# A graph layer on one core: rows of B made from nodes in the order they lie, and the rest of the prologue beside a larger first chunk

## The chip, the cores and the metric

The kernel runs on one core of one Trainium2 chip. The metric is the device time of one execution in microseconds (us). The engines are PE (TensorE: matmuls; its weight loads are listed apart as PEld), DVE (VectorE), ACT (ScalarE), POOL (GpSimd) and SP (SyncE, which here only issues transfers). ACT and POOL issue transfers as well. Each engine works through its own list of instructions in order.

## What is computed

A graph network layer with a normalisation ahead of it and a residual sum behind it, on 12,500 nodes of 64 features and 212,500 edges that are sorted by `dst`:

```python
h = jnp.maximum(_layernorm(x, axis=-1), 0.0)
edge_in = jnp.concatenate([h[row], h[col], dist], axis=1)     # row = src, col = dst
e = jax.nn.silu(edge_in @ eW1 + eb1)
e = jax.nn.silu(e @ eW2 + eb2)
agg = jax.ops.segment_sum(e, row, num_segments=h.shape[0])
node_in = jnp.concatenate([h, agg], axis=1)
out = jax.nn.silu(node_in @ nW1 + nb1) @ nW2 + nb2
return x + out
```

The weights are 129 x 128 (eW1), 128 x 128 (eW2), 192 x 128 (nW1) and 128 x 64 (nW2); all are float32.

## The kernel before

The first edge layer is split: `h[src] @ eW1[:64] + eb1` is the table A (`ta`), `h[dst] @ eW1[64:128]` the table B (`tb`), one row per node, each row stored as three bfloat16 parts that add up to the float32 value. Nodes are kept in buckets: node n belongs to bucket n mod 100 at place n / 100, so a partition holds 100 consecutive nodes.

**Prologue (L201 to L319).** All of x is loaded with 100 consecutive nodes in a partition. For five groups of 20 buckets the norm is computed (L234 to L248), then for every four buckets the transposes (L252), the matmuls, and the three parts of B's rows (`product`, L169 to L192, called with s=1). Beside it the edge lists are prepared: for each pair of blocks the lowest `dst` (L267), the offset of each edge from it, bucket and place of each `src` (L282 to L293), the three parts of the edge weights (L298), and transposed copies (L301 to L313). `rows`, `aux`, the table `tb` and the transposed norms `hd` are written to HBM. The framework schedules this part.

**Blocks and chunks.** A block is 1024 edges. For each block `load` fetches `bc` (the offsets and buckets, copied to all partitions), a window of 112 rows of `tb`, and `pick` (edge weights). `count` (DVE) marks each edge's row and bucket and ranks the edges of a bucket by a running sum (L400). `send` multiplies the window by the marks (L435: 24 matmuls), copies the result to `qs`, and POOL scatters 128 rows at a time with an indirect transfer (L454) into a list `q` in HBM that is sorted by bucket of `src`. There are 208 blocks, eight scatters each (1661 in all). Blocks come in chunks, and each chunk has its own `q`: `CHUNKS` at L49 gives pairs of blocks, tiles of 128 rows per bucket and the rows that need no zero fill. Before, the first chunk has 8 blocks and one tile per bucket, and ten chunks of 20 blocks and two tiles follow. The fill of the next chunk's list is issued on ACT's queue (L96).

**Steps.** The lists are read back per four buckets (a batch; `fetch`, L489) together with A's rows. A step handles four tiles of 128 edges: mark the place of each edge (L521, L526), transpose the rows and add A's (L535, L542), Silu, second edge layer (L573), Silu, and sums per node (L587). One tile per bucket gives one step per batch, two tiles give two, so there are 525 steps in both versions.

**The order.** From L363 on the order of PE, DVE, ACT and SP is written out by hand. Ahead of the steps, `send_all(0)` sends the first chunk's blocks (L642). In the loop at L658 each turn calls the stages of several steps in the order of `turn` (L605), which has four hooks (`None`). At a hook pieces of the next chunks' blocks are run, three pieces to a block. `marks` spreads the pieces evenly over the hooks between two bounds: chunk c has to be sent when batch c x 25 - 5 is worked off, as its first batches are fetched then. A's rows are made by `feeds` (L623): `hd` is read back four buckets at a time, two calls of `next(feed)` per piece in the first chunk, then one per hook. `fetch` waits for a batch's A rows.

**Last chunk.** With its batches, `node_in` loads x and `hd`, and after a batch's sums `nodes` (L333) computes the node layers of four buckets, one stage per hook: two matmuls each into `z` (L341, L342), Silu, `o` (L346 adds the bias by a matmul with ones, L348), the sum with x (L351) and the store.

Of the kernel before, what the change touches and what calls it, by code (L numbers as in the profile page):

```python
# [48 lines left out]
CHUNKS = [(4, 1, 48)] + 10 * [(10, 2, 152)]  # L49
# [8 lines left out]
def tile_gnn(ctx: ExitStack, tc: tile.TileContext, x, src, dst, ew, eW1, eb1, eW2, eb2, nW1, nb1, nW2, nb2, out):  # L58
# [44 lines left out]
    CH = 20  # L103
    x_rows = x.rearrange("(l b) d -> l b d", b=NB)
# [24 lines left out]
    nb2r = const.tile([1, G, D], F32, name="nb2r")  # L129
    for t in range(G):  # L130
        nc.gpsimd.dma_start(nb2r[:, t, :], rows_of(nb2, 1))
# [35 lines left out]
    tables = [t.rearrange("(l b) f -> l b f", b=NB) for t in (ta, tb)]  # L167

    def product(s, b0, hr, ps, tag, sb, sb2, queue):  # L169
# [22 lines left out]
        queue.dma_start(tables[s][:, b0 : b0 + G, :], parts.rearrange("p b s f -> p b (s f)"))  # L192
# [4 lines left out]
    base_i = const.tile([1, 2, NP], I32, name="base_i")  # L197
    NW = 4
    wins = [const.tile([P, 3, H], BF16, name=f"win{i}") for i in range(NW)]

    with tc.tile_pool(name="pro", bufs=1) as pro, tc.tile_pool(name="norm", bufs=2) as np_, tc.tile_pool(  # L201
        name="nab", bufs=2
    ) as nab, tc.tile_pool(name="nps", bufs=2, space=PSUM) as nps:
        xs = pro.tile([P, NB, D], F32, name="xs")
        for c0 in range(0, NB, CH):
            nc.vector.memset(xs[96:, c0 : c0 + CH, :], 0.0)
            rows16(nc.sync.dma_start, xs[:, c0 : c0 + CH, :], x_rows[:, c0 : c0 + CH, :])
        for f in fill(0, nc.sync, NB):
            f()


        srcR = pro.tile([NP, PAIR], I32, name="srcR")
        dstR = pro.tile([NP, PAIR], I32, name="dstR")
        ewR = pro.tile([NP, PAIR], F32, name="ewR")
        pad_i = pro.tile([1, PAD], I32, name="pad_i")
        nc.gpsimd.memset(pad_i, N)
        pad_f = pro.tile([1, PAD], F32, name="pad_f", tag="pad_i")
        nc.gpsimd.memset(pad_f, 0.0)
        vec = lambda v, lo, n, m: bass.AP(tensor=v.tensor, offset=v.offset + lo, ap=[[m, n], [1, m]])
        for to, v, pad in (  # L220
            (dstR, dst, vec(dst, E - PAD, 1, PAD)),
            (srcR, src, pad_i),
            (ewR, ew, pad_f),
        ):
            for p0, p1 in ((0, NP // 16 * 16), (NP // 16 * 16, NP - 1)):
                nc.scalar.dma_start(to[p0:p1, :], vec(v, p0 * PAIR, p1 - p0, PAIR))
            nc.scalar.dma_start(to[NP - 1 : NP, :LAST], vec(v, (NP - 1) * PAIR, 1, LAST))
            nc.scalar.dma_start(to[NP - 1 : NP, LAST:], pad)


        hT = pro.tile([P, NB // 2, P], F32, name="hT")
        for c0 in range(0, NB, CH):
            xc_ = xs[:, c0 : c0 + CH, :]
            mean = np_.tile([P, CH], F32, name="mean")  # L234
            nc.vector.tensor_reduce(mean, xc_, AX.X, OP.add)
            nc.vector.tensor_scalar(mean, mean, 1.0 / D, None, op0=OP.mult)
            cen = np_.tile([P, CH, D], F32, name="cen")
            nc.vector.tensor_tensor(cen, xc_, mean[:, :, None].to_broadcast([P, CH, D]), op=OP.subtract)
            sq = np_.tile([P, CH, D], F32, name="sq")
            nc.scalar.activation(sq, cen, AF.Square)  # L240
            var = np_.tile([P, CH], F32, name="var")
            nc.vector.tensor_reduce(var, sq, AX.X, OP.add)
            nc.vector.tensor_scalar(var, var, 1.0 / D, EPS, op0=OP.mult, op1=OP.add)
            nc.scalar.activation(var, var, AF.Sqrt)
            nc.vector.reciprocal(var, var)
            nc.vector.scalar_tensor_tensor(
                xc_, cen, 0.0, var[:, :, None].to_broadcast([P, CH, D]), op0=OP.max, op1=OP.mult
            )  # L248
            for b0 in range(c0, c0 + CH, G):
                ht = nps.tile([P, G // 2, P], F32, name="ht")  # L250
                for i in range(G // 2):
                    nc.tensor.transpose(  # L252
                        ht[:, i, :], xs[:, b0 + 2 * i : b0 + 2 * i + 2, :].rearrange("p j d -> p (j d)"), ident
                    )
                hr = hT[:, b0 // 2 : b0 // 2 + G // 2, :]
                nc.scalar.copy(hr, ht)
                for _ in product(1, b0, hr, nps, "ab", nab, nab, nc.sync):
                    pass
            nc.sync.dma_start(hd[:, c0 // 2 : (c0 + CH) // 2, :], hT[:, c0 // 2 : (c0 + CH) // 2, :])


        rowsS = pro.tile([NP, 2, 2, BLK], BF16, name="rowsS")
        f = pro.tile([NP, PAIR], F32, name="f")
        nc.scalar.copy(f, dstR)
        fv = f.rearrange("p (g e) -> p g e", g=2)
        lo = pro.tile([NP, 2], F32, name="lo")
        nc.vector.tensor_reduce(lo, fv, AX.X, OP.min)  # L267
        nc.vector.tensor_scalar(lo, lo, float(N - WL), None, op0=OP.min)
        hi = pro.tile([NP, 2], F32, name="hi")
        nc.vector.tensor_reduce(hi, fv, AX.X, OP.max)  # L270
        lot = nps.tile([1, 2, NP], F32, name="lot", tag="tr")
        for g in range(2):
            nc.tensor.transpose(lot[:, g, :], lo[:, g : g + 1], ident[:NP, :NP])
        nc.vector.tensor_copy(base_i, lot)
        nc.vector.tensor_tensor(hi, hi, lo, op=OP.subtract)
        nc.vector.tensor_scalar(hi, hi, WL - 0.5, None, op0=OP.is_gt)
        nc.vector.tensor_reduce(bad[:NP, 0:1], hi, AX.X, OP.max)
        nc.vector.tensor_tensor(
            rowsS[:, :, 0, :], fv, lo[:, :, None].to_broadcast([NP, 2, BLK]), op=OP.subtract
        )  # L280

        sf = pro.tile([NP, PAIR], F32, name="sf", tag="f")  # L282
        nc.scalar.copy(sf, srcR)
        t = pro.tile([NP, PAIR], F32, name="t")
        nc.vector.tensor_scalar(t, sf, 0.5, 1.0 / NB, op0=OP.add, op1=OP.mult)
        ti = pro.tile([NP, PAIR], I32, name="ti", tag="dstR")
        nc.vector.tensor_copy(ti, t)
        lc = pro.tile([NP, PAIR], F32, name="lc")
        nc.scalar.copy(lc, ti)
        nc.vector.tensor_tensor(t, lc, t, op=OP.is_gt)  # L290
        nc.vector.tensor_tensor(lc, lc, t, op=OP.subtract)
        nc.vector.scalar_tensor_tensor(sf, lc, -float(NB), sf, op0=OP.mult, op1=OP.add)
        nc.scalar.copy(rowsS[:, :, 1, :], sf.rearrange("p (g e) -> p g e", g=2))  # L293
        nc.sync.dma_start(rows, rowsS)

        auxS = pro.tile([NP, 2, 3, BLK], BF16, name="auxS")
        ev = ewR.rearrange("p (g e) -> p g e", g=2)
        parts3(pro, auxS[:, :, 0, :], auxS[:, :, 1, :], auxS[:, :, 2, :], ev, [NP, 2, BLK], tag="t")  # L298
        nc.sync.dma_start(aux, auxS)


        for what, (of, to) in enumerate(((sf, bkE), (lc, locE))):
            for k0 in range(0, 2 * TB, 4):
                tr = nps.tile([P, 4, NP], F32, name="tr")
                for k in range(4):
                    nc.tensor.transpose(tr[:, k, :], of[:, (k0 + k) * P : (k0 + k + 1) * P], ident[:NP, :NP])
                if what:
                    nc.scalar.add(to[:, k0 : k0 + 4, :], tr, 1.0)
                else:
                    nc.scalar.copy(to[:, k0 : k0 + 4, :], tr)  # L310
        for p0, p1, cap, _, _ in chunks:
            v = bkE[:, :, p0:p1]
            nc.vector.tensor_scalar(v, v, float(cap * P), -1.0, op0=OP.mult, op1=OP.add)  # L313


        d3 = pro.tile([P, 3, H], BF16, name="d3")
        parts3(pro, d3[:, 0, :], d3[:, 1, :], d3[:, 2, :], w1d, [P, H])
        for win in wins:
            nc.sync.dma_start(win[WL : WL + 3, :, :], d3[:3, :, :])  # L319

    aggp = ctx.enter_context(tc.tile_pool(name="aggp", bufs=1))
    aggT = aggp.tile([P, NB, L], F32, name="aggT")
    out_rows = out.rearrange("(l b) d -> l b d", b=NB)

    def nodes_in(B, sb):
        b = B * G
        xr = sb.tile([L, G, D], F32, name="xr")
        rows16(nc.sync.dma_start, xr, x_rows[:, b : b + G, :])
        hr = sb.tile([P, G // 2, P], F32, name="hrn")
        nc.sync.dma_start(hr, hd[:, b // 2 : b // 2 + G // 2, :])  # L330
        return xr, hr

    def nodes(B, xr, hr, ps, sb, tag):  # L333
# [13 lines left out]
        for t in range(G):  # L347
            nc.tensor.matmul(o[:, t, :], zs[:, t % 2, t // 2, :], w2n, start=False, stop=t == G - 1)  # L348
# [474 lines left out]
```

## Time and profile before

| | |
|---|---|
| three runs, us | 2708.69, 2707.8, 2714.96 (median 2708.69) |
| profiled execution | 2708.9 us, of which the span from first to last instruction is 2706.9 |
| mean granted TensorE clock | 0.915 of full |
| PE busy | 2321.1 us (86%) |
| DVE busy | 1846.2 us (68%) |
| ACT busy | 1204.1 us (44%) |
| POOL busy | 1723.0 us (64%), of it 1710.3 in 1661 scatters |
| moved by DMA | 612.85 MB, mean 226 GB/s |
| first scatter, last scatter | start at 172.1 and 2417.6 us |

How to read it: busy time is summed over the span, so an engine at 64% may still be full in a stage. A row of the groups of instructions gives line, engine, operation, output and inputs, shapes and count, then busy us and mean ns of one, then idle time of the engine just ahead of them and what ended it. "issue" is time in which the engine waited for nothing that the profile shows. In the timeline the first number of a row is the start, the second the length of the run of instructions. PEclk is the clock granted to TensorE, as a share of full speed.

### The profile page before, as it was taken

What the parts mean: (1) busy time and instruction counts of PE and PEld (TensorE: products, weight loads), DVE (VectorE), ACT (ScalarE), POOL (GpSimd) and SP (SyncE); (2) the same over time, 40 slices, a digit from 0 to 9 for tenths busy, and PEclk for the clock granted to TensorE, in tenths of its full rate; (3) what the DMA queues carried; (4) which work ended last, traced back from release to release, by engine and by line L of the source; (5) the groups of instructions that cost most, each with busy time, mean ns of one, the idle gap of its engine ahead of it and who ended that gap; (6) DMA issues with size and microseconds to landing.
All of it is one profiled execution on the core that took longest, in us unless ns stands there. A gap on an engine that the chain in (4) does not pass through costs nothing. (4 is left out here: it accounts for less than half of the span.)

```text
span 2706.9 us, 61144 instructions
## 1 busy us (share of the span) xinstructions
PE 2321.1 (86%) x23583; PEld 2168.2 (80%) x23583; DVE 1846.2 (68%) x3287; ACT 1204.1 (44%) x2247; POOL 1723.0 (64%) x1691
## 2 busy tenths in 40 slices
PE   1656688799799699799979979979979979979998
PEld 0445577799699699799879979979979979978886
DVE  5745468688588588678768768868858868743332
ACT  2522234355355355355445435535535545534442
POOL 1036577777777777777777777777777777750000
PEclk9755689899899899999989989989989989989998
DMA  6477867987787697697797787788688758644441
GB/s 180 170 210 208 246 226 227 284 276 231 237 280 244 211 288 247 200 312 245 214 293 254 224 274 252 246 247 269 229 248 272 244 185 267 216 173 127 137 128 33
DMA packets 388692, 612.85 MB, mean 226 GB/s; under 512 B 47232, under 2 KB 294401, under 8 KB 387877
## 3 DMA queue, kind: packets, MB, share of 16 engines
q1 hardware_dynamic: 269560, 423.47, 48.7%
q0 software_dynamic: 53760, 122.94, 13.3%
q10 hardware_dynamic: 65074, 62.46, 9.4%
q8 instruction: 188, 3.08, 0.5%
q14 instruction: 110, 0.90, 0.1%
HBM read 393.49 MB, written 215.18 MB: 225 GB/s over the span
## 5 line engine op out<-in xcount | busy, mean ns | idle before, releaser
L454 POOL DMA_INDIRECT q<-qs,to x1661 | 1710.3, 1030 | 679.2 <-issue 386.4
L546 ACT ACTIVATE e<-pt 128x512 f32<-128x512 f32 x525 | 313.7, 597 | 926.5 <-PE pt L542 765.1
L573 PE MATMUL p<-w,e 128*128 128x128 f32 x4200 | 578.7, 282 | 102.3 <-ACT p L567 102.3
L573 PEld LDWEIGHTS p<-w,e 128*128 128x128 f32 x4200 | 523.6, 196 | 117.1 <-ACT p L567 104.3
L526 DVE TENSOR_SCALAR oneT<-lr,part 125x512 bf16<-125x512 f32 x525 | 392.3, 747 | 325.8 <-PE lr L521 325.7
L587 PE MATMUL seg<-one,e 128*128 128x125 f32 x4200 | 581.2, 282 | 19.8 <-DVE aggT L598 14.6
L587 PEld LDWEIGHTS seg<-one,e 128*128 128x128 f32 x4200 | 523.6, 196 | 22.6 <-ACT qs L442 11.7
L400 DVE TENSOR_TENSOR_SCAN run<-oh,end,misc 100x1024 f16<-100x1024 f16 x197 | 461.1, 2340 | 6.4 <-PE misc L427 5.8
L542 PE MATMUL pt<-oneT,a 125*128 125x256 bf16 (+1 forms) x3300 | 440.1, 272 | 0.0
L435 PE MATMUL qp<-win,pick 115*128 115x128 bf16 x4983 | 369.1, 227 | 37.1 <-DVE oneT L526 30.4
L442 ACT COPY qs<-qp 128x512 f32<-128x512 f32 x416 | 243.3, 585 | 286.5 <-PE qp L435 218.3
L435 PEld LDWEIGHTS <-pick 115*128 115x128 bf16 x4983 | 330.4, 102 | 45.3 <-issue 40.8
L553 DVE TENSOR_TENSOR one<-nodes,qt 128x500 f32<-128x500 f32 x525 | 352.2, 671 | 0.7 <-PE seg L587 0.5
L542 PEld LDWEIGHTS <-a 125*128 125x128 bf16 x3300 | 317.8, 99 | 33.5
L535 PE MATMUL pt<-ident,qt 128*128 128x128 f32 x2100 | 329.5, 281 | 3.1 <-DVE prest L187 2.2
L577 ACT ACTIVATE e<-p 128x512 f32<-128x512 f32 x525 | 313.2, 597 | 12.9 <-PE p L573 9.6
L567 ACT COPY p<-b2f 128x512 f32<-128x512 f32 x525 | 311.8, 594 | 0.0
L598 DVE TENSOR_TENSOR aggT<-aggT,seg 128x500 f32<-128x500 f32 x250 | 168.2, 673 | 152.5 <-PE seg L587 152.3
L521 PE MATMUL lr<-identb,qt 128*125 128x128 bf16 x2100 | 210.6, 224 | 62.2 <-DMA qt<-q 62.2
L521 PEld LDWEIGHTS <-qt 128*125 128x125 bf16 x2100 | 187.2, 140 | 64.0 <-DMA qt<-q 63.3
L535 PEld LDWEIGHTS pt<-ident,qt 128*128 128x128 f32 x2100 | 227.6, 144 | 4.0 <-DVE prest L187 2.3
L408 DVE TENSOR_TENSOR run<-run,oh 100x1024 f16<-100x1024 f16 x208 | 144.3, 694 | 7.1
(118 smaller groups left out, 1264.4 us busy)
## 6 DMA issues: line engine op xcount, KB each, us to landing
qt<-q SPq DMA_DIRECT2D x250, 576.0 KB
a<-ta SPq DMA_DIRECT2D x275, 384.0 KB
bc<-rows SPq DMA_DIRECT2D x208, 448.0 KB
q<-zeros ACTq DMA_DIRECT2D x40, 1462.5 KB
q<-qs,to POOLq DMA_INDIRECT x1661
win<-tb SPq DMA_DIRECT2D x208, 84.0 KB
tb<-parts SPq DMA_DIRECT2D x25, 384.0 KB
ta<-parts SPq DMA_DIRECT2D x25, 384.0 KB
```

The lines of the kernel that those rows point to most:

```text
L400: nc.vector.tensor_tensor_scan(run, oh, nil.to_broadcast([NB, BLK]), carry.get(c, 0.0), op0=OP.add, op1=OP.add)
L435: nc.tensor.matmul(qp[:, t, :], pick[: WL + 3, (t0 + t) * P : (t0 + t + 1) * P], win[: WL + 3, i, :], start=i == 0, stop=i == 2,)
L454: i = nc.gpsimd.indirect_dma_start(out=q[:], out_offset=bass.IndirectOffsetOnAxis(ap=to[:k, t : t + 1], axis=0), in_=qs[:k, t - t0, :], in ...
L521: nc.tensor.matmul(lr[:L, t, :], loc[:, at : at + 1].to_broadcast([P, L]), identb, start=True, stop=True)
L526: nc.vector.tensor_scalar(oneT, st[k].pop("lr")[:L], part1[:L, :], None, op0=OP.is_equal)
L535: nc.tensor.matmul(pt[:, t, :], qt[:, j, :H], ident, is_transpose=True, start=t == 0, stop=False, skip_group_check=True)
L542: nc.tensor.matmul(pt[:, cols, :], a3[:L, b, i, :], oneT[:, cols, :], start=False, stop=i == 2, skip_group_check=True)
L546: nc.scalar.activation(e1, pt, AF.Silu)
L553: nc.vector.tensor_tensor(one, nodes1[:, None, :].to_broadcast([P, G, L]), qt[:, j : j + G, H : H + 1].to_broadcast([P, G, L]), op=OP.is_e ...
L573: nc.tensor.matmul(p2[:, t, :], e1[:, t, :], w2, start=False, stop=t == G - 1, skip_group_check=True)
L577: nc.scalar.activation(e2, p2, AF.Silu)
L587: nc.tensor.matmul(item[2][:, b, :], e2[:, t, :], one[:, t, :], start=j % n == 0, stop=j % n == n - 1)
```

## The change

- `CHUNKS`: the first chunk has 20 blocks and two tiles per bucket (168 rows of each list need no fill), the second is the one with 8 blocks and one tile, nine of 20 follow.
- x is loaded in the order in which nodes lie: tile j holds nodes 128 j to 128 j + 127, a node per partition. `norm` and `products` make B's rows of 20 tiles. Those of the first 20 tiles are written twice, to `tb` and to `tb0`; the first 24 blocks take their windows from `tb0`, whose end also bounds their lowest `dst`.
- Ahead of the first block are only the norm and B's rows of the first 20 tiles and the edge lists (`lists`), in an order written out by hand, as everything is now. The lowest `dst` of a block is that of its first edge, and bucket and place are found in fewer passes.
- The other four groups of norms and B rows, the checks that were in the prologue, and all of A's rows (`head`) run beside the blocks of the first chunk, four `next(feed)` per piece; what is left is run ahead of the steps. Normed nodes go to HBM (`hn`), and A's rows are made from them after they are read back in buckets, 20 at a time; `hd` is written then.
- In the loop nothing of A is left (`next(feed)` and the wait in `fetch` are gone). `b2f` is made after the first chunk is sent.
- Node layers: both `z` are opened first (two matmuls with `w1g`), then the two with `w1n`, then both Silus. `nb2` is added to x by POOL when x is loaded, in place of the matmul with ones.

```diff
-CHUNKS = [(4, 1, 48)] + 10 * [(10, 2, 152)]
+CHUNKS = [(10, 2, 168), (4, 1, 48)] + 9 * [(10, 2, 152)]
...
+    NT = 100
+    EARLY = 24
...
-    for t in range(G):
-        nc.gpsimd.dma_start(nb2r[:, t, :], rows_of(nb2, 1))
+    nb2b = const.tile([P, D], F32, name="nb2b")
+    nc.gpsimd.dma_start(nb2b, rows_of(nb2, P))
...
-        queue.dma_start(tables[s][:, b0 : b0 + G, :], parts.rearrange("p b s f -> p b (s f)"))
+        for table in [tb_tiles, tb0_tiles][: 1 + (b0 < CH)] if s else [ta_buckets]:
+            queue.dma_start(table[:, b0 : b0 + G, :], parts.rearrange("p b s f -> p b (s f)"))
...
+        nc.gpsimd.tensor_tensor(xr, xr, nb2b[:L, None, :].to_broadcast([L, G, D]), op=OP.add)
...
+        z = [ps.tile([P, G // 2, L], F32, name="z", tag=tag) for _ in range(2)]
+        for a in range(2):
+            nc.tensor.matmul(z[a], w1g, aggT[:, b + a : b + G : 2, :], start=True, stop=False)
         for a in range(2):
             half = slice(a * D, (a + 1) * D)
-            z = ps.tile([P, G // 2, L], F32, name="z", tag=tag)
-            nc.tensor.matmul(z, w1g, aggT[:, b + a : b + G : 2, :], start=True, stop=False)
-            nc.tensor.matmul(z, w1n[half, :], hr[half, :, :L], start=False, stop=True)
-            nc.scalar.activation(zs[:, a], z, AF.Silu, bias=nb1c)
+            nc.tensor.matmul(z[a], w1n[half, :], hr[half, :, :L], start=False, stop=True)
+        for a in range(2):
+            nc.scalar.activation(zs[:, a], z[a], AF.Silu, bias=nb1c)
...
-        nc.tensor.matmul(o, ones[:, :L], nb2r, start=True, stop=False)
         for t in range(G):
-            nc.tensor.matmul(o[:, t, :], zs[:, t % 2, t // 2, :], w2n, start=False, stop=t == G - 1)
+            nc.tensor.matmul(o[:, t, :], zs[:, t % 2, t // 2, :], w2n, start=True, stop=True)
...
+                table, end = (tb0, CH * P) if s < EARLY else (tb, N)
...
-            while B not in done_a:
-                next(feed)
...
+        def norm(j0, xs):
...
+            nc.sync.dma_start(xs[:, :full, :], rows_[: full * P, :].rearrange("(j p) d -> p j d", p=P))
...
+            yield
+            mean = nm.tile([P, CH], F32, name="mean")
+            nc.vector.tensor_reduce(mean, xs, AX.X, OP.add)
...
+            yield
+            nc.vector.reciprocal(var, var)
...
+            nc.sync.dma_start(hn.rearrange("(j p) d -> p j d", p=P)[:, j0 : j0 + CH, :], xs)
+            yield
+
+        def products(s, j0, g, xs):
+
+            ht = mm.tile([P, G // 2, P], F32, name="ht", tag="mm")
+            for i in range(G // 2):
+                nc.tensor.transpose(
+                    ht[:, i, :], xs[:, g + 2 * i : g + 2 * i + 2, :].rearrange("p j d -> p (j d)"), ident
+                )
             hr = wk.tile([P, G // 2, P], F32, name="hr")
+            nc.scalar.copy(hr, ht)
+            if s == 0:
+                nc.sync.dma_start(hd[:, (j0 + g) // 2 : (j0 + g + G) // 2, :], hr)
+            yield
+            yield from product(s, j0 + g, hr, mm, "mm", wk, wk, nc.sync)
...
+        def head():
+
+            for j0 in range(CH, NT, CH):
+                xs = xsp.tile([P, CH, D], F32, name="xs")
+                yield from turns([norm(j0, xs)], 1)
+                yield from turns([products(1, j0, g, xs) for g in range(0, CH, G)], 3)
+            yield from checks()
+            for b0 in range(0, NB, CH):
+                xs = xsp.tile([P, CH, D], F32, name="xs")
+                nc.sync.dma_start(xs, hn.rearrange("(l b) d -> l b d", b=NB)[:, b0 : b0 + CH, :])
+                yield
+                yield from turns([products(0, b0, g, xs) for g in range(0, CH, G)], 3)
...
+            xs = xsp.tile([P, CH, D], F32, name="xs")
+            first_norm = norm(0, xs)
+            next(first_norm)
...
+            for _ in first_norm:
+                pass
+            for z in fill(0, nc.sync, NB):
+                z()
...
+            for _ in turns([lists()] + [products(1, 0, g, xs) for g in range(0, CH, G)], 3):
+                pass
+            load(0, 1)
+            load(1, 1)
+            for _ in count(0):
+                pass
+            feed = head()
+            for _ in send_all(0):
+                for _ in range(4):
+                    next(feed, None)
+            for _ in feed:
+                pass
...
-                    next(feed, None)
```

`turns(todo, width)` runs up to `width` of the listed pieces of work in rotation, and hands control back after each part of one.

## The prediction

> **What bounds the kernel now.** I read, in this order: the groups of instructions by line, GpSimd's scatters by stretches of time, GpSimd's timeline, the granted clock and busy time in the same stretches, then the last stage's timeline.
>
> In the list of groups one line fills GpSimd (POOL):
>
> ```profile
> L454 POOL DMA_INDIRECT q<-qs,to x1661 | 1710.3, 1030 | 679.2 <-issue 386.4
> ```
>
> 1661 scatters of 1.03 us with mostly 0.30 us of issue between them, one after the other. By stretches (busy us of PE, PEld, DVE, ACT, POOL; granted clock; DMA share; GB/s):
>
> ```profile
> 172.00:260.00 88.00, 65.43 (x369) 47.19 (x367) 46.14 (x92) 21.93 (x46) 64.59 (x64) 0.54 0.77 216
> 260.00:500.00 240.00, 178.94 (x1672) 157.17 (x1672) 152.01 (x287) 79.71 (x156) 166.10 (x159) 0.79 0.75 233
> 500.00:2420.00 1920.00, 1738.00 (x19214) 1693.28 (x19214) 1449.74 (x2585) 928.56 (x1708) 1479.65 (x1439) 0.95 0.78 246
> 2420.00:2707.00 287.00, 270.10 (x2001) 221.50 (x2001) 95.18 (x156) 107.71 (x204) 0.00 (x0) 0.96 0.38 121
> ```
>
> From 500 to 2420 POOL does 1439 scatters in 1920 us, 1.33 each: with its 0.30 between them it is full, while PE has 182 us to spare. After 2420 there is no scatter, and PE alone works off the last chunk. GpSimd's timeline gives the ends:
>
> ```profile
> 172.13 1.17 POOL L454 DMA_INDIRECT q<-qs,to  x1 [143.24 <-ACT qs L442]
> ...
> 500.99 0.97 POOL L454 DMA_INDIRECT q<-qs,to  x1 [0.30 <-issue]
> ...
> 2417.58 0.88 POOL L454 DMA_INDIRECT q<-qs,to  x1 [0.30 <-issue]
> ```
>
> The 64th scatter (end of the first chunk) starts at 258.9, the 160th near 413, the 224th (end of the second chunk) at 501.0 by count. So the time is: start of the first scatter, plus 1661 scatters, plus whatever POOL stands idle, plus the last stage. After the change the first two chunks again hold 224 scatters (160 + 64), and nine chunks of the old size follow, which took 2417.6 - 501.0 = 1916.6. I keep that figure: PE needs less there than POOL (below). So I compare one point, the start of the 224th scatter, and the last stage.
>
> **A turn of PE.** In the last stage without node work a turn repeats every 3.115 us (a weight load of L573 at 2434.03, 2437.14, 2440.26). In full-PE stretches (1400 to 1500) 100 us hold 26.6 turns and 75 scatters (9.4 blocks): (100 - 26.6 x 3.115) / 9.4 = 1.8 us of PE per block. Twenty blocks beside 50 turns want 156 + 36 = 192 us, POOL 20 x 8 x 1.33 = 213.
>
> **1. The first scatter.** x for the first 20 tiles (0.66 MB) lands near 9 us (0 to 30 moved 208 to 276 GB/s). ScalarE waits in order for the pads: their memset stood at 19.94 behind four nb2r loads (1.9 us, 3.0 of waits); with one load about 17, four issues of 0.3 to 0.9 end near 20. Table loads and squares (1.28, 1.26), sums, root and scaling (1.48, 0.17, 1.5, 0.27, 1.48) end at 26.5. The row lists: cast 1.9, lo 0.2, difference 2.29, then three passes of 1.22 and one of 2.29, cast 1.9: rows issued near 40; aux, 4 x 1.9 to 2.3, near 49. What is gone there: three passes and a cast of 1.2 to 2.3 and two reductions of 2.28 (these go to the checks). SP's queue, though, carries the zero fill first: 88 x 576 B x 100 = 5.1 MB from 27 to about 49 at 230 GB/s; rows land near 53. The five groups of B write 2 x 393 KB each out of two `parts` buffers, so the third waits for the first one's landing; before this wait cost 19.5 us in the prologue:
>
> ```profile
> L183 ACT CAST parts<-ab 128x256 bf16<-128x256 f32 x52 | 17.1, 376 | 41.4 <-PE ab L182 21.3 <-DMA tb<-parts 19.5 <-ACT parts L188 0.6
> ```
>
> Five groups in two-buffer steps of about 5 us from 54 make tb0 complete near 78. Three block loads (2 to 5 us apart at 154 to 161) put the second x load at 85 to 90, landed 95. In VectorE's order the second norm (6.5 us, 1.8 of waits) and the scan (2.3) stand ahead of the first `to`: first scatter at **106**, bounds 98 to 115, against 172.1. By then only the first fifth of B's rows and two of the five norms are done, and no A row; the rest is the price.
>
> **2. The head: 20 blocks with the rest beside them.** Four `next(feed)` per piece, three pieces per block, 12 per block; four norm-and-B rounds of 24, 12 for the checks, five A rounds of 21.
> - *B rounds* last 8 blocks, three norms of them after the first scatter. VectorE per block: 0.48 + 0.52 + 2.34 + 0.15 + 0.69 + 0.14 + 2 x 0.20 = 4.7. Busy: 8 x 4.7 + 3 x 6.5 + 20 groups x (0.76 + 0.69) = 86. Waits: the mean stands in VectorE's queue right behind the load that SP issues only after the last `parts` write, and behind it stand the next scan, `to` and the group's halves, for which POOL waits: 6 us (a 0.46 MB `bc` took 4.9 at 146) x 3; squares and root 1.8 x 3; `parts` landings 0 to 1.5 x 20, taken 0.75; 4 odd. Sum 86 + 18 + 5 + 15 + 4 = **128** (115 to 145), 16 per block where POOL wants 10.9 (86.8 us for 64).
> - *Checks*: 4.7 + two reductions of 2.3 + 12 small ones = **12**.
> - *A rounds*, 25 groups over 8.75 blocks. Near 172 a group's L180 and L182 matmuls took 4.6 (166.31 to 170.9 at the clock of 0.5), its two transposes 0.55, a block's 24 qp and 8 rank matmuls 3.1: 25 x 5.15 + 8.75 x 3.1 = 156 at the clock of 0.54. VectorE needs only 77. Five loads of `xs` from `hn`, each used by PE at once, drain the three groups in flight (5 + 3 us each); against that the clock will be above 0.5 at times. Taken: **160**, bounds 125 (at full clock a group took 2.5 near 225: 25 x 2.8 + 8.75 x 1.8 + 40) to 200 (156 + 40, rounded).
> - *The last 2.25 blocks* at POOL's pace: **24**.
>
> The row is the clock of 0.54 with PE busy 65 of 88. The Trainium skill (TensorE: Matmul & The Clock Gate, "The HAM clock gate") says that one window of about 3.4 us sustained work releases the clock; by it a continuously busy A phase would run at full clock and the sum would be 35 lower. I let the row decide.
>
> 160th scatter: 106 + 128 + 12 + 160 + 24 = **430**, where before had it at 413.
>
> **3. Chunk 1: eight blocks over 43 turns.** The marks spread 24 pieces over 172 hooks, because chunk 0 now has two steps per batch. Landing and fetch 6 (258.9 to lr at 264.3 was 5.4); three turns of filling 6; cold clock 3; 40 turns x 3.115 = 125; 8 x 1.8 = 15; the last scatters 5: **160**. POOL needs 85 of it. The b2f matmuls (3.8 us, moved here) lie under the fetch; uncovered they cost 4. 224th scatter: 590, against 501.0: **+89**.
>
> Chunk 2 then has 29 turns for its 20 blocks (126 us of PE, POOL 213): bound by POOL, as is everything after it, so no lead of PE comes back.
>
> **4. Last stage.** Two turns with a node layer take 10.39 us, all of it PE:
>
> ```profile
> 2651.27 0.59 PE L341 MATMUL z<-aggT,w1g 128*128 128x250 f32 x2
> 2651.79 0.69 PE L342 MATMUL z<-hrn,w1n 64*128 64x250 f32 x2
> 2652.41 0.69 PE L341 MATMUL z<-aggT,w1g 128*128 128x250 f32 x2
> 2653.03 0.69 PE L342 MATMUL z<-hrn,w1n 64*128 64x250 f32 x2
> 2653.64 1.16 PE L573 MATMUL p<-w,e 128*128 128x128 f32 x8
> 2654.73 0.69 PE L346 MATMUL o<-nb2r,ones 1*125 1x256 f32 x2
> 2655.35 1.08 PE L348 MATMUL o<-w2n,zs 128*125 128x64 f32 x8
> ```
>
> L346 goes: 2655.35 - 2654.73 = 0.62, and 0.04 to 0.1 around it: 25 x 0.66 = 16.5. The two L342, now adjacent on different halves, may overlap: 0 to 0.62 each; the nearest rows (L182's two halves, 0.12 per pass like whole ones) show none, so I take a quarter: 4. Together **-20** (-16 to -32). The Trainium skill (TensorEngine Tiling, "Key Properties") says tiles on different rows execute in parallel; by it the gain here would be 32. The 25 additions on GpSimd are in no row: between a memset of 0.58 and five times that; POOL has nothing after its last scatter and a node layer comes 20 us later, so 0; uncovered, one of them (up to 3) ahead of the first node layer.
>
> **Sum.** 2708.9 (profiled: span 2706.9 and 2.0 around it; median 2708.7) + 89 - 20 = **2778 us**, +2.6%. Its own range is 2730 to 2815.
>
> **Rivals.**
> - *Faster: POOL keeps its pace in the head.* If waits of VectorE and PE overlap and nothing delays a block, 20 blocks take 217 from 106: 160th at 323, 224th at 483, -18 - 20: 2671. For it: VectorE has 20 x 10.9 - 20 x 4.7 = 123 us free beside the blocks and the added work is 20 + 29 + 36 + 7 = 92; the 56 MB moved (scatters 11.8, bc 9.2, ta 9.8, tb 7.9, x, hn and hd 11.2, fill 4.6, win 1.7) would need 259 GB/s, seen elsewhere (263 at 1400 to 1500). Against: in-order queues with a load awaited at once, nine times. It decides below 12.6 us per block (break-even: 224th at 521, 160th at 361).
> - *Nothing gained or lost*: A warm and waits half hidden, 160th near 361: 2709.
> - *Worse*: A cold with all waits (200), B at 145: 160th at 487, 224th at 647: 2835.
>
> **How the numbers follow.** My case 0.52, faster 0.20, no change 0.08, worse 0.20. Within 0.3% (2700.6 to 2717) is about what a measurement of this kernel cannot tell from no change. The range 2685 to 2815 leaves out half of the faster case and half of the worse one.
>
> **What would show it.** Right: first scatter 98 to 115; norms in VectorE's queue preceded by idle time ending on the `xs` load; 14 us or more per block in the head; 160th near 430; POOL idle over 60 us of the next 160 with PE full; from there 1917 to the last scatter; period of a node layer 9.6 to 9.75. Wrong: the 160th before 361, or the eight blocks done in under 120 us, or nine chunks that take other than 1900 to 1935.

## The result, and the profile after

The changed kernel takes **2794.5 us** (median of four runs, 2791.3 to 2798.2) beside 2708.2 for the kernel before: a ratio of 1.032, 95% interval 1.030 to 1.034. The profiled execution took 2791.3 us, its span is 2789.5, 82.6 more than before.

In the list of groups GpSimd's scatters are still 1661 and as long as before (1.03 us), but the idle time ahead of them has grown from 679 to 820 us:

```profile
L348 POOL DMA_INDIRECT q<-qs,to x1661 | 1704.1, 1026 | 819.7 <-issue 433.4
```

GpSimd's timeline shows where: the first scatter, the last one of the chunk of 20 blocks and the one behind it, the last one of the chunk of 8, and the very last. The bracket is the idle time ahead and what ended it.

```profile
115.90 1.06 POOL L348 DMA_INDIRECT q<-qs,to  x1 [97.05 <-ACT parts L188]
...
470.24 0.97 POOL L348 DMA_INDIRECT q<-qs,to  x1 [0.30 <-issue]
485.04 1.48 POOL L348 DMA_INDIRECT q<-qs,to  x1 [13.83 <-ACT qs L336]
...
623.83 0.96 POOL L348 DMA_INDIRECT q<-qs,to  x1 [0.30 <-issue]
...
2541.75 0.88 POOL L348 DMA_INDIRECT q<-qs,to  x1 [0.30 <-issue]
```

Read as a sum along GpSimd's stream (starts, us), this is the whole difference:

| stretch | before | after | difference | foretold |
|---|---|---|---|---|
| to the first scatter | 172.1 | 115.9 | -56.2 | -66 |
| first to 160th | 241.7 | 354.3 | +112.7 | +83 |
| 160th to 224th | 87.2 | 153.6 | +66.4 | +73 |
| 224th to last | 1916.6 | 1917.9 | +1.3 | 0 |
| last scatter to the end | 289.3 | 247.8 | -41.6 | -20 |
| span | 2706.9 | 2789.5 | +82.6 | +69 |

The head's waits stand in VectorE's queue: of the three norms after the first scatter, each begins with idle time that ends when its rows of x have landed (28.3 us in all; here two of them).

```profile
148.62 1.49 DVE L513 TENSOR_REDUCE mean<-xs 128x20 f32<-128x1280 f32 x1 [13.12 <-DMA xs<-in_x_dram]
...
188.23 1.49 DVE L513 TENSOR_REDUCE mean<-xs 128x20 f32<-128x1280 f32 x1 [7.53 <-DMA xs<-in_x_dram]
```

The A rounds (A's rows of 20 buckets at a time), by stretches of 20 us (the columns: window, its length, busy us of PE, PEld, DVE, ACT, POOL; granted clock; DMA share; GB/s), and below them the stretch in which the eight blocks of chunk 1 are sent:

```profile
300.00:320.00 20.00, 19.76 (x78) 12.94 (x78) 7.05 (x15) 6.14 (x15) 4.90 (x6) 0.50 0.32 107
...
340.00:360.00 20.00, 20.00 (x80) 13.13 (x79) 8.56 (x17) 6.21 (x15) 6.17 (x6) 0.50 0.37 124
...
485.00:624.00 139.00, 139.00 (x1469) 135.88 (x1468) 98.03 (x170) 74.42 (x138) 66.34 (x64) 1.00 0.80 250
```

Two stages with TensorE full and GpSimd far from full: in the first TensorE is full at *half* its clock (in the stretches between these it stands 5 to 7 us, waiting for `hn`; over 262 to 446 it is busy 157 of 184 us, all at 0.50), in the second at full clock. The last stage, one node layer and the start of the next (times of the first column):

```profile
2732.66 1.01 PE L226 MATMUL z<-aggT,w1g 128*128 128x250 f32 x4
2733.61 0.69 PE L229 MATMUL z<-hrn,w1n 64*128 64x250 f32 x4
2734.23 1.16 PE L465 MATMUL p<-w,e 128*128 128x128 f32 x8
...
2741.43 0.80 PE L226 MATMUL z<-aggT,w1g 128*128 128x250 f32 x3
```

The two L229, on different halves of the array, now take 0.62 us together (2733.61 to 2734.23), as long as one took before. The period of a node layer is 8.77 us (2732.66 to 2741.43), before 10.39.

### The profile page after: what moved, and what is told of

It reads as the page before. It is cut to its first block, busy times and chain, and to the rows that moved or that the text cites. A ratio compares the mean times of both kernels' runs of the same rounds, so it can differ in the third digit from the quotient of the medians.

```text
span 2789.5 us, 61343 instructions
## 1 busy us (share of the span) xinstructions
PE 2315.8 (83%) x23583; PEld 2174.3 (78%) x23583; DVE 1845.0 (66%) x3286; ACT 1209.1 (43%) x2271; POOL 1733.5 (62%) x1713
## 4 chain that ended last, share of the span: by engine, by line
PE 57%; DMA 13%; POOL 6%; issue 3%; DVE 3%; ACT 1%; ACTq 0%; SPq 0%; DVEq 0%; POOLq 0%
PE seg L479 14%; PE p L465 13%; DMA q<-qs,to 10%; PE pt L434 10%; PE pt L427 7%; PE qp L329 7%; POOL q L348 6%; PE lr L413 3%; DMA qt<-q 1%; PE misc L321 1%; PE z L226 1%; PE o L235 1%; DMA win<-tb 1%; DVE run L294 1%; PE z L229 1%
## 5 line engine op out<-in xcount | busy, mean ns | idle before, releaser
L479 PEld LDWEIGHTS seg<-one,e 128*128 128x128 f32 x4200 | 522.7, 196 | 41.6 <-ACT qs L336 25.3
L329 PE MATMUL qp<-win,pick 115*128 115x128 bf16 x4983 | 377.9, 230 | 36.2 <-DVE oneT L418 22.6
L329 PEld LDWEIGHTS <-pick 115*128 115x128 bf16 x4983 | 337.4, 104 | 45.6 <-issue 29.3
```

What stands on the lines that cost most here:

```text
L329: nc.tensor.matmul(qp[:, t, :], pick[: WL + 3, (t0 + t) * P : (t0 + t + 1) * P], win[: WL + 3, i, :], start=i == 0, stop=i == 2,)
L479: nc.tensor.matmul(item[2][:, b, :], e2[:, t, :], one[:, t, :], start=j % n == 0, stop=j % n == n - 1)
```

## Experiments

The theory that the experiments test: the time is the start of the 224th scatter, plus 1917, plus the last stage; the loss is GpSimd's idle time in the head (awaited loads, a cold TensorE) and beside chunk 1 (the marks). Rivals are in each expectation. Starts and lengths are us in the profiled execution:

| kernel | 1st | 160th | 224th | last | last to end | median | ratio to before (95%) |
|---|---|---|---|---|---|---|---|
| before | 172 | 414 | 501 | 2418 | 289 | 2708 | |
| after | 116 | 470 | 624 | 2542 | 248 | 2794 | 1.030 to 1.034 |
| e1_nodes | 172 | 416 | 503 | 2422 | 248 | 2671 | 0.982 to 0.986 |
| e7_order_alone | 175 | 387 | 541 | 2466 | 288 | 2753 | 1.011 to 1.016 |
| e3_pace | 117 | 469 | 564 | 2485 | 249 | 2736 | 1.006 to 1.010 |
| e4_ahead | 114 | 425 | 578 | 2499 | 250 | 2750 | 1.011 to 1.015 |
| e11_pace_ahead | 113 | 423 | 519 | 2444 | 248 | 2689 | 0.989 to 0.993 |
| e12_all_full_rows | 111 | 351 | 451 | 2369 | 249 | 2620 | 0.964 to 0.968 |

The kernels e2, e5, e6, e8, e9 and e10 met chips on which the kernel before itself took some 3415 us (there all engines stand in short idle times for which the trace names no cause), so of them only stretches are read, beside each other. Beside e1, e3, e4 and e7 it took 2713.7, beside e11 and e12 2709.9; the ratios are to these.

### One part alone: the node layers

The edits of `nodes` and `nodes_in`, made in the kernel before (the z matmuls are rearranged as the change does it):

```diff
+        nc.gpsimd.tensor_tensor(xr, xr, nb2b[:L, None, :].to_broadcast([L, G, D]), op=OP.add)
...
+        for a in range(2):
+            nc.tensor.matmul(z[a], w1g, aggT[:, b + a : b + G : 2, :], start=True, stop=False)
...
-        nc.tensor.matmul(o, ones[:, :L], nb2r, start=True, stop=False)
```

> The kernel before with only the node layers rearranged (no nb2 matmul, z matmuls with equal weights side by side); prologue, chunk order and head as before. Theory (the change's time is first scatter + idle of GpSimd + 1917 + last stage, and the four parts add up): first scatter 172, 224th 501, last scatter 2417, all as before; only the node layer's period falls from 10.39 to 8.77 us as it did in the changed kernel, 25 x 1.62 = 40.5: 2668 us (2664 to 2673). Rival A, the sizes of the prediction (nb2 16.5, a quarter of the overlap): 2688. Rival B, that the last stage of the changed kernel is shorter for another reason (its chunks, its tables as they lie): less than 10 us gained, 2699 or more.

Measured 2671.2, and 248.2 us from the last scatter to the end. The theory holds: these edits alone are worth 41 us in the last stage (289.3 before), and they would have made the kernel before 1.6% faster. To split them, the same without the z order:

> The kernel before with only the nb2 matmul taken away (nb2 added to xr by GpSimd), the z matmuls in their old order. Splits the 40 us of the node layers. Theory (one 1-row matmul of 0.62 us per node layer, 25 of them; the rest of the 40 belongs to the z order, where two half-height matmuls run at the same time): 16 us gained, 2692 beside a before of 2708, a period of 9.75. Rival (the missing matmul also frees a buffer or a wait and carries most of the 40): 30 us or more gained.

Its last stage has TensorE full as elsewhere, and e5, e6 and e8 have the changed kernel's period of 8.77 on the same chip, so its period can be read there (two z matmuls, one node layer apart):

```profile
3302.71 0.59 PE L341 MATMUL z<-aggT,w1g 128*128 128x250 f32 x2
...
3312.28 0.59 PE L341 MATMUL z<-aggT,w1g 128*128 128x250 f32 x2
```

9.57 against 10.39 and 8.77: the missing matmul is worth 0.82 a layer (20 us in all; its own length is 0.62, I had 0.66 with what lies around it), the z order 0.80 (20), of which 0.62 is the overlap of the two L229; the rest lies in the two matmuls with `w1g`, 0.95 side by side and 0.52 and 0.62 apart. Most of my error is in the second, where I had 4.

### One part alone: the order of the chunks

In the kernel before:

```diff
-CHUNKS = [(4, 1, 48)] + 10 * [(10, 2, 152)]
+CHUNKS = [(10, 2, 168), (4, 1, 48)] + 9 * [(10, 2, 152)]
```

> The kernel before with only the order of the chunks changed (20 blocks first, then 8, then nine times 20); prologue with all of B, A beside the first chunk and node layers as before. Theory (the order itself costs: A must be done before the first fetch and 8 blocks are spread over 43 turns of TensorE): first scatter 172 plus up to 5 for a larger zero fill, 160th at 410 to 425, 224th at 565 to 590 (501 before), time 2775 to 2797. Rival (the loss of the changed kernel is all in the head, norms and B beside the blocks, and the order is free): 224th near 501 to 515, time within 12 us of 2709.

Its 160th and 224th scatter in GpSimd's timeline:

```profile
386.54 0.97 POOL L454 DMA_INDIRECT q<-qs,to  x1 [0.30 <-issue]
...
540.51 0.97 POOL L454 DMA_INDIRECT q<-qs,to  x1 [0.30 <-issue]
```

Slower by 39 us than the kernel before in its group (2713.7), the direction right, the size not: the eight blocks of chunk 1 took 154 us as in the changed kernel, but the 20 blocks before them only 211.5, GpSimd's own pace (1.33 each). So A's rows, spread over 20 blocks (their first write at 176, the last at 396), cost GpSimd nothing, though from 200 to 350 TensorE is busy 139 of 150 us at a clock of 0.51. In the changed kernel they are pressed into under ten blocks (276 to 446), because B's rounds come first.

### Chunk 1: the marks

```diff
-            marks.append((hooks * (by - first), total))
+            if c > 1:
+                marks.append((hooks * (by - first), total))
```

> The changed kernel with one mark less: the pieces of the second and third chunk (28 blocks) are spread evenly over the passes of the first two chunks (288 hooks), where the changed kernel spreads 8 blocks over 172 hooks and then 20 over 116. Theory (GpSimd idles beside the second chunk because the marks give it 8 blocks in 154 us of full TensorE, and the idle time never comes back): 72 turns x 3.115 + 28 x 1.8 = 275 us of TensorE against 224 x 1.33 = 298 of GpSimd, so GpSimd paces it: 384th scatter at 783 to 800 (837 in the changed kernel), time 2740 (2735 to 2760). Rival (TensorE, not the marks, is what the 28 blocks wait for, or the loads of whole 576 KB batches collide with the scatters): 384th scatter stays above 825, time within 12 us of 2794.

Its 161st, 224th and 384th scatter:

```profile
479.73 0.97 POOL L348 DMA_INDIRECT q<-qs,to  x1 [9.99 <-issue]
564.46 1.17 POOL L348 DMA_INDIRECT q<-qs,to  x1 [0.30 <-issue]
782.46 0.97 POOL L348 DMA_INDIRECT q<-qs,to  x1 [0.30 <-issue]
```

303 us for 28 blocks where the changed kernel took 353 (485.0 to 837.9), and 2736 instead of 2794: right to a few us (the 384th came at 782, one short of the 783 to 800 expected). The idle time beside chunk 1 is not what TensorE needs for eight blocks; it comes of one line that hands out eight blocks per 43 turns.

### The awaited loads

In `head`; `begin` takes a tile and runs the first step of `norm`, its load. The reads of `hn` are moved ahead likewise:

```diff
-                xs = xsp.tile([P, CH, D], F32, name="xs")
-                yield from turns([norm(j0, xs)], 1)
+                xs, work_ = ready
+                yield
+                yield from turns([work_], 1)
+                if j0 + CH < NT:
+                    ready = begin(j0 + CH)
                 yield from turns([products(1, j0, g, xs) for g in range(0, CH, G)], 3)
```

> The changed kernel with every xs load of the head issued one round ahead of its use (the second x load right behind the first scatter's norm, each later one behind the norm before it, each read of hn one round ahead). Theory (the awaited load, 28 us in the three norms after the first scatter and 25 us in the A rounds, is on the path of the head): 64th scatter at 235 or earlier (257.7), 160th at 440 or earlier (470.2), time 2755 (2745 to 2770). Rival (the cold TensorE and the norms' own 6 to 9 us of VectorE set the head, the waits lie under them): 160th scatter after 458, time within 12 us of 2794.

The second norm in VectorE's timeline, with no idle time ahead of it:

```profile
135.61 1.48 DVE L513 TENSOR_REDUCE mean<-xs 128x20 f32<-128x1280 f32 x1
```

The next two norms start without a wait, too. 64th scatter at 237.7 (257.7), 160th at 424.8 (470.2), 2750 us. The theory holds, though the 64th is 3 us later than it asked for. The A rounds now last 157 us (243 to 400) with TensorE busy 155 of them, all at a clock of 0.50: what is left of this stage is the cold TensorE.

### The clock in A's rounds

For A in `product`; eb1f holds eb1 in row 0 and zeros below, ones_f ones in 128 rows, w1z one half of w1 and zeros for the other half:

```diff
-                nc.tensor.matmul(ab, ones, eb1r, start=True, stop=False)
+                nc.tensor.matmul(ab, ones_f, eb1f, start=True, stop=False)
...
+                    nc.tensor.matmul(ab[:, i], hr[:, i, :], w1z[:, a, :], start=False, stop=i == G // 2 - 1)
```

> The changed kernel with the matmuls of A's rows on all 128 rows of the array: w1's half padded with zero rows (64 rows before), eb1 as row 0 of an otherwise zero tile under 128 rows of ones (1 row before); as many matmuls of the same shapes of output. Theory (the granted clock stays at 0.5 beside a busy TensorE because most of its work there uses 1 or 64 of 128 rows): clock above 0.9 from 300 to 440, a matmul pair 0.62 instead of 1.22, A rounds 40 to 60 us shorter, time 2745 (2730 to 2755). Rival (rows have nothing to do with it; the clock answers to the short gaps and to the blocks' own matmuls): clock 0.50 still, time within 10 us of 2794.

Two stretches of A's rounds, columns as in the same view of the changed kernel above:

```profile
300.00:320.00 20.00, 12.55 (x98) 10.89 (x96) 10.55 (x23) 7.25 (x18) 10.42 (x11) 0.83 0.55 190
...
340.00:360.00 20.00, 12.64 (x114) 10.39 (x112) 14.57 (x28) 8.69 (x21) 11.20 (x11) 0.93 0.62 219
```

Clock 0.62 to 0.93 from 280 to 420, 0.78 over the A rounds (274 to 416) with TensorE busy 90 of 142 us. The changed kernel stood at 0.50 with TensorE busier, and so did the next kernel, e6, on the same chip with the old matmuls (0.51 from 265 to 450). The theory holds in kind, not in size: one stretch of seven is above 0.9, and from 420 on it is 0.50 again. 160th scatter at 445.9, against 475.4 for e6; what of that is due to the chip is open, so I take its time from the last experiment.

### The fill

```diff
+            for z in fill(0, nc.gpsimd, NB):
+                z()
...
-            for z in fill(0, nc.sync, NB):
-                z()
```

> The changed kernel with the first chunk's zero fill issued from GpSimd's queue, ahead of the first norm, instead of SP's. Theory (the fill kept SP's queue until 57.95, and rows, aux and the writes of B were late by that): rows issued near 41 instead of 57.95, tb0 written by 75 instead of 86, first scatter at 103 (98 to 108) instead of 115.9, time 2783 (2776 to 2790). Rival (the bytes, not the queue, are the limit, or the fill from this queue is slower than the first scatter allows): first scatter at 114 or later, time 2790 or more.

SP's queue in the changed kernel (start, us):

```profile
28.28 2.31 SPq L96 DMA_DIRECT2D q<-zeros  x1
30.68 27.16 SPq L674 DMA_DIRECT2D win<-d  x4
57.95 0.38 SPq L584 DMA_DIRECT2D rows<-rowsS  x1
```

And with the fill from GpSimd's:

```profile
28.95 25.89 SPq L673 DMA_DIRECT2D win<-d  x4
54.95 0.38 SPq L584 DMA_DIRECT2D rows<-rowsS  x1
```

The rival is nearer: with the fill out of SP's queue the four small writes still stand until 54.8, `rows` is issued 3 us earlier, and the first scatter comes at 113.4 (114 or later for the rival, 108 at most for the theory). So the place in the queue explains 3 us at most. The same four writes in the kernel before, issued 85 us after its fill, took 3 us:

```profile
86.25 2.91 SPq L319 DMA_DIRECT2D win<-d  x4
```

The long stand thus goes with a fill under way. That the fill's bytes are the limit is argued, not shown: in e6 the DMA share is 0.9 to 1.0 from 20 to 50, and I tried no kernel with a smaller fill.

### Everything together

Besides the loads a round ahead, in e8, e9, e10 and e12 both first chunks are sent in the head, and one mark stands for all the others (e11 joins only the edits of e3 and e4):

```diff
-            for _ in send_all(0):
-                for _ in range(4):
+            for _ in itertools.chain(send_all(0), send_all(1)):
+                for _ in range(3):
                     next(feed, None)
...
-            marks.append((hooks * (by - first), total))
+        marks.append((hooks * (by - first), total))
```

> The changed kernel with xs loaded a round ahead as before, and with both first chunks (28 blocks) sent in the head, three steps of the head's other work per piece instead of four; the other nine chunks are spread evenly over all the turns (0.38 blocks per turn). Theory (GpSimd is the bound once it is given blocks at its own pace; the head's other work of some 300 us then lies beside 224 scatters that need 298): 224th scatter at 445 (430 to 470; 578 with the loads ahead alone), a gap of 15 to the next, then 1437 x 1.334 = 1917, last stage 248: 2627 (2605 to 2650). Rival (TensorE, cold in the head and a chunk behind after it, becomes the bound of the passes): nine chunks take over 1950, time above 2660.

> The same kernel as in the second group (28 blocks in the head, xs a round ahead, nine chunks spread evenly), once more beside a kernel before that takes its usual 2709. Theory: the nine chunks are bound by GpSimd again, 1917 to 1925 from the 224th scatter to the last; the head ends where the second group had it or a little earlier (224th scatter at 480 to 506), last stage 248: 2650 to 2680. Rival (TensorE becomes the bound of the passes, being a chunk behind): over 1950 for the nine chunks, above 2690.

> As the run beside it, and A's rows made with all 128 rows of the array (zero-padded w1) and eb1 put into PSUM by ScalarE's copy instead of a 1-row matmul, which took 2.4 of a group's 5.2 us at the clock of 0.5. Theory (the second half of the head is bound by TensorE at half its clock on thin matmuls): clock above 0.7 in A's rounds, the blocks beside them at GpSimd's 10.7 us each, 224th scatter 40 to 60 us earlier than in the run beside it (430 to 450), time 2600 to 2630. Rival (the awaited norms, parts landings and in-order queues set the head, not TensorE): less than 15 us earlier.

These three met the slow chips; the head reads 64th, 160th, 224th scatter at 219, 390, 506 (e8, and e9 within 1), 220, 393, 512 (e10). e10 leaves A's rows incomplete (most likely eb1's share, copied ahead of the matmuls, is missing from some); its instructions are those of a kernel that would have them whole. Halving TensorE's work there brought nothing, as the rival had it, but this is no test of what bound e8: the edit put a new wait ahead of the matmuls, for that copy (total us, times, longest; 255 to 470):

```profile
PE ab L192 <- ACT ab L189: 74.5, 41, 11.8
```

My 445 for e8 was 60 too early; what bound its head stays open. The clock of e10 stayed at 0.50 to 0.59 from 240 to 460 with full rows and TensorE busy 7 to 13 of 20 us, so full rows alone don't raise it. The last two ran where the kernel before took 2710:

> Both repairs of the first group in one kernel: xs loads a round ahead in the head, and the pieces of the second and third chunk spread evenly over two passes. Beside a kernel before at 2709. Theory (the time is a sum along GpSimd's stream, so the two add): 160th scatter at 425 as with the loads ahead alone, then 10 to 15 of gap, then 2005 to the last scatter as with the even spread alone, then 248 to 250: 2696 (2688 to 2704), a ratio of 0.990 to 0.998. Rival (both fill the same idle time, or the earlier blocks meet a busier TensorE): 2715 or more. Beside a chip on which the kernel before takes 3400 no verdict on the time is possible; then only the start of the 160th scatter is read.

2689 (ratio 0.991): the two repairs add up (-58 and -45 from 2794 would be 2691).

> 28 blocks in the head, xs a round ahead, the nine other chunks spread evenly, and A's matmuls on all 128 rows. Beside a kernel before at 2709. Theory: 64th scatter at 220 to 236, 160th at 365 to 385 (389 without full rows), 224th at 460 to 485 (506 without), granted clock above 0.6 in A's rounds, then 1917 and 248: 2640 to 2665, a ratio of 0.975 to 0.984. Rival (the head is set by in-order queues, not by TensorE's clock): 160th at 385 to 392, 224th at 500 or later, 2675 or more; if TensorE becomes the bound of the nine chunks, over 1950 for them. Beside a chip on which the kernel before takes 3400 only the head is read.

Two stretches of A's rounds, the middle of them (columns as above; over all of them, 256 to 401, the clock is 0.79, from 0.66 to 0.96 in stretches of 20 us, and TensorE is busy 94 of 145 us):

```profile
300.00:320.00 20.00, 15.06 (x131) 12.86 (x131) 15.52 (x31) 9.60 (x23) 15.30 (x15) 0.93 0.89 291
320.00:340.00 20.00, 16.66 (x139) 14.34 (x137) 13.26 (x32) 8.48 (x20) 15.63 (x15) 0.85 0.70 217
```

One pair of A's matmuls there:

```profile
323.83 0.60 PE L195 MATMUL ab<-eb1f,ones_f 128*128 128x256 f32 x2
324.26 0.61 PE L198 MATMUL ab<-w1z,hr 128*128 128x128 f32 x4
```

And the 160th, 224th and last scatter:

```profile
350.94 0.96 POOL L361 DMA_INDIRECT q<-qs,to  x1 [0.30 <-issue]
...
451.09 0.97 POOL L361 DMA_INDIRECT q<-qs,to  x1 [0.30 <-DMA pick<-aux]
...
2369.07 0.88 POOL L361 DMA_INDIRECT q<-qs,to  x1 [0.31 <-issue]
```

**2620 us, faster than both kernels** (0.966 of before, 0.964 to 0.968), and 20 better than the theory's best. In these two stretches GpSimd is busy 15.3 to 15.6 of 20 us, its full pace; L195 and L198 start 0.43 apart where the old pair lay 1.15 apart (339.54, 340.69 in the changed kernel); and nine chunks take 1918.0 again. How much of the step from 2689 is the 28 blocks and how much the full rows was not tried apart on such a chip. The parts of the change are thus worth having: e11, which only places the same work differently, is 105 us faster than the changed kernel and 0.9% faster than the kernel before. What cost the change 86 us was where the work was put.

## Why the prediction was right, step by step

The forecast of 2778 and its mechanism held (a head of 17.7 us a block, GpSimd idle beside chunk 1 with TensorE full, 1917 from there); 2794 lies inside the case's own range. That the profiled run's 2791 lies only 13 us above it is in part luck: in the order below the terms missed by 10, 18, -12, 24, -6 and -22 us, which nearly cancel. The first scatter, the B rounds and the last stage fell outside the bounds that were given for them. By its terms:

- **The bound and the 1917.** Right: 1917.9 after, 1918 to 1925 in every kernel on a chip like the first one.
- **First scatter, 106; it was 115.9.** Rows were issued near 58 and not near 40, behind four small writes that I had left out; I had them land at 53, and bc could be issued only at 64.1. From there the steps are as foretold: the third group waits 18.4 us on `tb<-parts` (19.5 in the row used), tb0 complete at 86 plus landing, the second x load issued at 98.4.
- **B rounds, 128; 146.** The three awaited norms cost 28.3 instead of 18, the landings of `parts` 20.3 instead of 15; the other 3 I can't name. e4 shows that the loads are to blame: with them ahead the 64th scatter comes 20 us earlier, 2 of them gained ahead of the first.
- **Checks, 12; none.** They ran at 253 to 263, beside the last blocks of the B rounds and the first load of `hn`.
- **A rounds, 160; 184** (262 to 446), inside 125 to 200. The clock stayed at 0.50 all the time, and 25.2 us of waits for `hn` lay open; I had let a clock above 0.5 at times make up for the waits. e4 takes these off and leaves 157, where the prediction's cold work was 156. e12 brings the stage to 145 (256 to 401). The 160th came at 470, 40 later than I had it: 10, 18, -12 and 24.
- **Chunk 1, 160; 153.6**, of which 14.8 are the step from one chunk to the next. e7 and e3 show the cause to be order and marks, as argued.
- **Last stage, -20; -41.6.** The term that failed: I took a quarter of the overlap of the two L342, and it is whole (16 of the 21.6 us that I missed); and the missing matmul is worth 0.82, not 0.66 (4). The Trainium skill (TensorEngine Tiling, "Key Properties") has tiles on different rows run in parallel, and here the trace agrees: 0.62 us for both. The rows that I had preferred, L182's halves before, I had read wrongly: they show the overlap too. At the same clock of 0.50 B's eight passes on both halves take as long as A's four on one half:

```profile
101.01 1.23 PE L182 MATMUL ab<-w,hT 64*128 64x128 f32 x8
...
168.60 1.22 PE L182 MATMUL ab<-w,hr 64*128 64x128 f32 x4
```

- **The clock.** The row decided against the rule, and rightly. The Trainium skill (TensorE: Matmul & The Clock Gate, "The HAM clock gate") ties the clock to how busy TensorE was in a window of some 3.4 us; here it stayed at 0.50 with TensorE busy 19.8 to 20 of 20 us, and rose to 0.93 in stretches with 12.6 to 15 of 20 once the matmuls used all rows (e5, e12; 0.78 and 0.79 over their A rounds). Busy time alone does not explain that; nor do full rows alone (e10, 0.51 from 255 to 470).
- **The rival "faster"** (GpSimd keeps its pace in the head) was not this kernel, but it was close by: e7 keeps the pace beside A's rows (1.33 us a scatter), e12 comes nearer to it beside everything (1.51 over the first 160, against 2.23 in the changed kernel).

## What to carry to other kernels

Where one engine's stream is the bound, write the time as the sum of its idle stretches and ask of each what hands it its work: here one line that sets how many blocks a turn gets cost 58 us (e3), and loads issued only when they were needed cost 45 (e4). Work moved out of a prologue was free where it was spread over enough of the bound engine's items (A's rows in e7), and cost less once every load that it awaits was issued a round ahead. Judge the parts of a change one by one: of this one, the node layers gained 41 us and the early start 56 while order and head lost 180.

## What the runs showed of the hardware that was not expected

- Thin matmuls and the clock: 1-row and 64-row fp32 matmuls, TensorE busy 20 of 20 us, clock 0.50; zero-padded to 128 rows, busy 12.6 to 16.7 of 20 in the stretches shown, clock 0.83 to 0.93 (0.78 and 0.79 over all A rounds of e5 and e12). A pair L195 and L198 takes 0.88 us (323.83 to the next start at 324.71) instead of 2.30, more than the clock's factor of two; in a cold moment of e12 it takes 1.71 (319.13 to 320.84). Padding with zeros was cheaper than leaving rows unused.
- Two 64-row matmuls on different halves of the array, side by side in the last stage at full clock: 0.62 us for both, 0.62 for each before. At the clock of 0.50 the same holds for L182: eight passes on both halves in 1.23 us, four on one half in 1.22.
- Four small DMAs issued beside a 5 MB fill stood 26 to 27 us in SP's queue, whether the fill was in SP's own queue or in GpSimd's; 3 us in the kernel before, long after its fill.
